# Summing key features against the context itself, and a new planner for the fills of two attention loops

## The chip, the cores and the metric

The kernel runs on one core of a Trainium2 chip. Times are device microseconds (us) of one execution. Five engines matter: TensorE (PE in the profile; its weight loads are PEld), VectorE (DVE), ScalarE (ACT), GpSimd (POOL) and the SyncE queue (SP), from which all DMAs are issued. Before the change three runs took 2615.45 to 2621.15 us, with a median of 2617.82.

## The reference

A perceiver of four levels: a stream x of 2 batches x 256 tokens x 256 features passes twelve blocks, some of which read a context of 2 x 4096 tokens x 256 features. Three blocks matter here.

`L0_xattn` and `L1_xattn` are ordinary cross attention with 16 heads of 16 features over all 4096 context tokens. They are where most of the time goes.

`L3_xattn` is linear attention of the stream on the same context:

```python
q, k, v = q @ Wq.T, k @ Wk.T, v @ Wv.T          # k and v are the context
q, k = focus(q), focus(k)                       # softmax(log(|leaky(x)|+eps) * factor) * mean
qh, kh = keep_11_largest_of_each_head_of_16(qh), ...(kh)
z_inv = einsum(qh, kh.mean(tokens)) + EPS
kv = einsum('bnc,bnd->bcd', kh / sqrt(n), vh / sqrt(n))
y = einsum('bnc,bcd->bnd', qh, kv) / z_inv
return y @ Wp.T
```

The keys' features of `L3_xattn` depend on the context and weights alone. So does kv, a sum over 4096 tokens of the product of the thinned key features and the values.

## The kernel before

Everything is fp32. The context's half of `L3_xattn` (class `Focus`) isn't computed in its own block but inside the two cross attention loops, one batch in each: `L0_xattn`'s loop does batch 0 and `L1_xattn`'s loop batch 1.

**A loop of steps.** `ContextAttention.attend` runs 8 units (2 batches x 4 groups of heads) of PER = 16 steps, and LAG and a last unit behind them, 148 steps in all. In step g PE does `first_scores` for one unit (L1018, eight PE instructions; DVE takes the maxima, L1026, two of 128 x 1024), then a **fill**, then `scores` for the unit 18 steps behind (L1042; ACT takes the exponents, L1052), then `weigh` of the step before (L1066). In steps 0 to 17 there are no second scores yet, in steps from 128 on no first ones. At the end of a unit, `weigh` copies the accumulator by DVE (L1075), and a step later `inverses` (L201) takes reciprocals.

**Banks.** PSUM in the loop has one bank for fills (`mm=1`), three pairs for scores (`sc=3`) and one accumulator. A step takes four pairs of the three in turn.

**Fills.** One step holds one fill at most: projecting keys (L939) or values (`v_ps`, L180), turning a unit's maxima (`shift_queries`, L994), normalising a unit, projecting one context tile of 128 tokens for `Focus` (`project`, L697: key features and values side by side, 512 columns), or adding up a chunk of four tiles (`add_up`, L710). `project` is followed by ACT (L609, and L701 which copies the values) and POOL (L610). When a chunk's four tiles are there, `Focus.weigh` takes the logarithm (ACT L617, POOL L618), the maximum (DVE L620), the exponents (L623) and a factor. Then `sparsify` ranks the 16 features of each head against each other: 15 shifts of one comparison (L648) and two additions (L650, L652) on DVE, then a select (L655) and a multiply by the factor (L660).

**Order.** PE, DVE and ACT follow the program's order here (`manual_schedule`). `plan` puts each fill into a step by due time, and holds for each step what DVE has left for ranking (`side`, 2.75 us with a fill, 2.0 without, minus what else falls there). `attend` hands out ranking instructions by that credit at the end of each step, behind `weigh`, `inverses` and the weighing. The sum of a chunk has a fixed step; if its ranking isn't over by then, all that is left of it is put out at once:

```python
if g in self.sums:
    run(rankings[self.sums[g]])
run(fills.get(g, ()))
```

The block `L3_xattn` (`l3_xattn`) does the same for its queries: projection, `weigh`, `sparsify`, transposes, then for each batch and half one product with kv and one with the features' sums, both masked to heads by `same`. It runs under the framework's own scheduling, not by program order.

Of the kernel before, what the change touches and what calls it, by code (L numbers as in the profile page):

```python
# [26 lines left out]
P = 128  # L27
# [556 lines left out]
class Focus:  # L584

    def __init__(self, net):
        self.net, self.nc = net, net.nc
        const, nc = net.const, net.nc  # L590
        src = net.ins["L3x_wkv"]
        self.wkv = const.tile(list(src.shape), F32, name="wkv", tag="wkv")
        nc.sync.dma_start(out=self.wkv, in_=src)
        self.power = net.vec("L3x_ff")
        self.eps = const.tile([P, 1], F32, name="eps6", tag="eps6")
        nc.gpsimd.memset(self.eps, 1e-6)
        self.rank0 = const.tile([P, P], BF16, name="rank0", tag="rank0")
        nc.gpsimd.iota(
            self.rank0, pattern=[[-1, DH], [0, H // ND]], base=DH - 1, channel_multiplier=0, allow_small_or_imprecise_dtypes=True
        )  # L600
        self.kv = [const.tile([P, ND, P + 1], F32, name=f"kv{b}", tag=f"kv{b}") for b in range(NB)]
# [30 lines left out]

    def sparsify(self, pool, y, factor):

# [9 lines left out]
        yield 0.42  # L644
        for s in range(1, DH):
# [3 lines left out]
            yield 0.13 + 1.18e-3 * N8 * n  # L649
            nc.vector.tensor_tensor(rank[:, :, P - n :], rank[:, :, P - n :], ge[:, :, :n], ALU.add)  # L650
            yield 0.13 + 0.62e-3 * N8 * n
            nc.vector.tensor_tensor(rank[:, :, :n], rank[:, :, :n], ge[:, :, :n], ALU.subtract)  # L652
            yield 0.13 + 0.62e-3 * N8 * n
# [4 lines left out]
        yield 1.22  # L658
        for t in range(NT):
            nc.vector.tensor_scalar_mul(y[:, t, :], y[:, t, :], factor[:, t : t + 1])  # L660
            yield 0.36


    def start(self, b, pool):
        self.b, self.pool, self.chunks, self.ctx, self.weighing = b, pool, [], [], []
        self.loads = iter([(kc, i) for kc in range(NKC) for i in range(2)])
        self.load()
# [11 lines left out]
    def project(self, kc, t):  # L679

        net, nc = self.net, self.nc
        if t == 0:
            y = self.pool.tile([P, NT, D], F32, name="fy", tag="fy")
            v = self.pool.tile([P, NT, ND, P + 1], F32, name="fv", tag="fv")
            nc.gpsimd.memset(v[:, :, :, P : P + 1], 1.0)
            total = net.sm(2, NT, name="f_total", tag="f_total")
            factor = net.sm(NT, name="f_factor", tag="f_factor")
            self.chunks.append((y, v, total, factor))
            self.weighing.append(self.weigh(y, total, factor))
        if t % 2 == 0:  # L690
            self.load()
        y, v, total, factor = self.chunks[kc]
        ctx = self.ctx[kc * 2 + t // 2]
        ps = net.mm("kv_ps")
        for d in range(ND):
            at = slice(t % 2 * P, (t % 2 + 1) * P)
            nc.tensor.matmul(ps, lhsT=ctx[:, d, at], rhs=self.wkv[:, d, :], start=d == 0, stop=d == ND - 1)  # L697
            if d < ND - 1:
                yield
        self.magnitudes(self.pool, y, total, t, ps[:, :D])  # L700
        nc.scalar.copy(v[:, t, :, :P], ps[:, D:].rearrange("p (m e) -> p m e", m=ND))  # L701

    def add_up(self, kc):

        nc = self.nc
        k, v, _, _ = self.chunks[kc]
        ps = self.net.mm("kv_sum")[:, : ND * (P + 1)].rearrange("p (m e) -> p m e", m=ND)
        for m in range(ND):
            for t in range(NT):
                nc.tensor.matmul(  # L710
                    ps[:, m, :], lhsT=k[:, t, m * P : (m + 1) * P], rhs=v[:, t, m, :], start=t == 0, stop=t == NT - 1
                )
            yield
        kv = self.kv[self.b]
        if kc == 0:
            nc.vector.tensor_copy(kv, ps)
        else:
            nc.vector.tensor_tensor(kv, kv, ps, ALU.add)


class ContextAttention:
# [73 lines left out]
    def plan(self):  # L795
# [6 lines left out]
        fills, todo, busy = {}, [], {}  # L802
        self.done = {}
        full, short = 2.75, 2.0
        side = [full] * STEPS
        for u in range(n):
            at = PER * (u + 1)
            fills[at] = self.shift_queries(u)
            side[at - 1] -= 0.3
            side[at] = short - 0.43  # L810
            at = PER * (u + 2) + LAG + 1
            self.done[at] = u
            side[at] -= 0.25
            if u < n - 1:
                fills[at + 1] = self.normalize(u)
                side[at + 1] = short - (0.43 if self.v_bias is None else 0.8)

        self.sums, self.weighings, self.rank_from = {}, {}, {}
        for kc in range(NKC):
            first = PER + 14 * kc + (2 if 2 * kc > NKC else 0)  # L820
            at = first + 28
            while at in fills:
                at += 1
            fills[at] = focus.add_up(kc)
            self.sums[at] = kc
            side[at] -= 0.45
            for t in range(NT):
                todo.append((first + 2 * t + 4, first + 2 * t + 1, focus.project(kc, t), kc))
        for j in range(self.begun, n * NKC // 2):
# [3 lines left out]
            last = max(4 * j - 8, 2 * i + PER + LAG + 1 if i >= 0 else 0)  # L833
            todo.append((4 * j - (5 if j < NKC // 2 else 3), last + 1, self.project_keys(j), -1))
        for b in range(NB):
            for kc in range(NKC):
                for k2 in range(2):
                    i = b * NKC + kc - self.VALUE_TILES
                    last = (i // NKC + 1) * NC16 * PER + LAG + 2 * (i % NKC) + 2 if i >= 0 else -1
                    first = (b * NC16 + 1) * PER + LAG + 2 * kc + k2  # L840
                    todo.append((first, last + 1, self.project_values(b, kc, k2), None))
        todo.sort(key=lambda t: t[0])
        for g in range((n + 1) * PER + LAG):

            ready = [t for t in todo if t[1] <= g and not (t[3] == busy.get(g - 1) == -1 and t[0] > g)]
            if g in fills or not ready:
                continue
            todo.remove(ready[0])
            assert ready[0][0] >= g, (g, ready[0])
            fills[g] = ready[0][2]  # L850
            busy[g] = ready[0][3]
        assert not todo


        for kc in range(NKC):
            done = max(g for g, of in busy.items() if of == kc)
            log = next((g for g in range(done + 1, done + 5) if g + 1 not in busy), done + 1)
            for behind in (0, 2, 3, 4, 5):
                self.weighings.setdefault(log + behind, []).append(kc)
            side[log + 2] -= 1.22  # L860
            side[log + 5] -= 0.65
            self.rank_from[kc] = log + 5
        for g in range(PER, STEPS):
            if g not in fills:
                side[g] += short - full
            if g >= n * PER:
                side[g] += 1.0
            if g >= 2 * PER + LAG and (g - PER - LAG - 1) % PER == PER - 1:
                side[g] -= 0.43
        self.side = side  # L870
        return fills

    def attend(self, vpool, ppool, fpool):
# [11 lines left out]
        rankings, ranked, credit = {}, 0, 0.0  # L885
        for g in range((n + 1) * PER + LAG + 2):
# [4 lines left out]
            if g in self.sums:  # L891
                run(rankings[self.sums[g]])
            run(fills.get(g, ()))
            if 0 <= second < n * PER:
# [9 lines left out]
            credit = min(credit, 0.5) + self.side[g]  # L904
            while ranked < NKC and self.rank_from[ranked] <= g:
                if ranked not in rankings:
                    y, _, _, factor = focus.chunks[ranked]
                    rankings[ranked] = focus.sparsify(fpool, y, factor)
                cost = next(rankings[ranked], None) if credit > 0.3 else 0.0
                if cost == 0.0:  # L910
                    break
                if cost is None:
                    ranked += 1
                else:
                    credit -= cost
# [1198 lines left out]
```

## Time and profile before

| what | value |
|---|---|
| median of three runs | 2617.82 us |
| the profiled execution | 2622.24 us, of which its span 2620.1 us |
| mean granted TensorE clock | 0.945 |
| busy shares of the span: PE, DVE, ACT, POOL | 90%, 61%, 41%, 13% |
| first loop, first scores of step 0 to first of step 127 | 35.9 to 675.1 us |
| second loop, the same | 999.5 to 1630.1 us |
| `project`, PE L697, both loops | 126.9 us busy in 256 instructions |
| `add_up`, PE L710, both loops | 34.4 us busy in 256 instructions |
| ranking, DVE L648, L650, L652 | some 400 us busy |

A PE instruction's own duration holds pipelining, so a group's busy time is more than the time it takes up on PE; the distance from one group's start to the next in the timeline is the better measure. A PE matmul in fp32 shows as two instructions. "Idle before" in a row tells how long the engine stood and who released it.

### The profile page before, as it was taken

What the parts mean: (1) busy time and instruction counts of PE and PEld (TensorE: products, weight loads), DVE (VectorE), ACT (ScalarE), POOL (GpSimd) and SP (SyncE); (2) the same over time, 40 slices, a digit from 0 to 9 for tenths busy, and PEclk for the clock granted to TensorE, in tenths of its full rate; (3) what the DMA queues carried; (4) which work ended last, traced back from release to release, by engine and by line L of the source; (5) the groups of instructions that cost most, each with busy time, mean ns of one, the idle gap of its engine ahead of it and who ended that gap; (6) DMA issues with size and microseconds to landing.
All of it is one profiled execution on the core that took longest, in us unless ns stands there. A gap on an engine that the chain in (4) does not pass through costs nothing.

```text
span 2620.1 us, 42454 instructions
## 1 busy us (share of the span) xinstructions
PE 2365.7 (90%) x16912; PEld 1222.9 (47%) x16920; DVE 1594.2 (61%) x2774; ACT 1069.4 (41%) x1891; POOL 332.8 (13%) x469
## 2 busy tenths in 40 slices
PE   7999999998998579999999999989999984789998
PEld 3444444544544354444445444554448442345453
DVE  4678888878846567488887788443231355434252
ACT  1355555555715132555555555531131352123241
POOL 3000011000024711000010000000011030002030
PEclk9999999999989789999999999978999996898989
DMA  5422222221010123322222220201222100000100
GB/s 184 141 82 86 66 78 82 70 79 57 2 37 33 46 81 120 99 82 74 70 79 91 75 72 18 80 13 49 85 97 89 37 17 13 33 20 12 51 16 20
DMA packets 89060, 165.99 MB, mean 63 GB/s; under 512 B 14704, under 2 KB 55280, under 8 KB 87968
## 3 DMA queue, kind: packets, MB, share of 16 engines
q1 hardware_dynamic: 88864, 163.29, 18.9%
q8 instruction: 134, 2.20, 0.3%
q14 instruction: 62, 0.51, 0.1%
HBM read 145.86 MB, written 0.59 MB: 56 GB/s over the span
## 4 chain that ended last, share of the span: by engine, by line
PE 49%; DVE 7%; ACT 2%; issue 1%; DMA 0%; POOL 0%; DVEq 0%; ACTq 0%; POOLq 0%
PE s L1042 5%; PE s L1018 5%; PE attn_acc L1066 5%; PE proj L180 4%; PE v_ps L180 3%; PE expert L180 2%; PE s L180 2%; PE kv_ps L697 2%; PE c_acc L1604 2%; PE ffn_ps L180 2%; PE k_ps L939 2%; DVE mx L1026 2%; PE s L1340 2%; PE kq_ps L180 1%; PE qk_ps L180 1%
## 5 line engine op out<-in xcount | busy, mean ns | idle before, releaser
L1026 DVE TENSOR_REDUCE mx<-s 128x2 f32<-128x1024 f32 x512 | 603.3, 1220 | 204.1 <-PE s L1018 202.6
L1052 ACT ACTIVATE p<-s 128x1024 f32<-128x1024 f32 x512 | 496.3, 1021 | 223.0 <-PE s L1042 219.0
L1042 PE MATMUL s<-xa_q,xa_k 32*128 32x256 f32 x4096 | 337.1, 405 | 36.9 <-DVE mx L1026 35.1
L1018 PE MATMUL s<-xa_k,xa_q 32*128 32x512 f32 x2048 | 350.7, 647 | 5.5 <-issue 2.8
L1042 PEld LDWEIGHTS s<-xa_q,xa_k 32*128 32x128 f32 x4096 | 207.4, 185 | 204.4 <-issue 118.5
L1066 PE MATMUL attn_acc<-p,xv 128*32 128x256 f32 x4096 | 278.9, 389 | 0.6 <-ACT p L1052 0.6
L1018 PEld LDWEIGHTS s<-xa_k,xa_q 32*128 32x128 f32 x2048 | 121.0, 185 | 123.5 <-issue 76.1
L648 DVE TENSOR_TENSOR ge<-fy 128x960 bf16<-128x960 f32 (+14 forms) x240 | 173.7, 724 | 6.4
L1066 PEld LDWEIGHTS attn_acc<-p,xv 128*32 128x32 f32 x4096 | 107.9, 109 | 132.2 <-issue 85.9
L610 POOL TENSOR_TENSOR fy<-fy,low 128x256 f32<-128x256 f32 x64 | 61.4, 960 | 697.0 <-ACT low L609 697.0
L697 PE MATMUL kv_ps<-wkv,f_ctx 128*128 128x512 f32 x256 | 126.9, 618 | 0.8 <-DVE xa_q L996 0.8
L650 DVE TENSOR_TENSOR rank<-rank,ge 128x960 bf16<-128x960 bf16 (+14 forms) x255 | 121.5, 476 | 6.8
L652 DVE TENSOR_TENSOR rank<-rank,ge 128x960 bf16<-128x960 bf16 (+14 forms) x255 | 111.3, 436 | 2.8
L387 POOL TENSOR_SCALAR p<-p,r 128x128 f32<-128x128 f32 (+1 forms) x192 | 82.5, 442 | 139.0 <-DVE r L383 76.2
L986 ACT COPY xv<-v_ps 128x512 f32<-128x512 f32 x64 | 37.5, 586 | 136.9 <-PE v_ps L180 127.0
L609 ACT ACTIVATE fy<-kv_ps 128x256 f32<-128x256 f32 x64 | 24.5, 383 | 149.9 <-PE kv_ps L697 149.9
L697 PEld LDWEIGHTS kv_ps<-wkv,f_ctx 128*128 128x128 f32 x256 | 43.3, 189 | 80.1 <-issue 71.4
L233 ACT ACTIVATE sq<-xc 128x512 f32<-128x512 f32 x24 | 14.6, 629 | 147.2 <-DVE xc L232 147.2
L368 ACT ACTIVATE p<-p,top 128x256 f32<-128x256 f32 (+1 forms) x128 | 57.1, 447 | 41.8 <-DVE top L356 39.0
L939 PE MATMUL k_ps<-ctx_k,w_L0x_wq 128*64 128x512 f32 x256 | 66.1, 619 | 3.0 <-DMA ctx_k<-in_ctxT 2.9
L1604 PE MATMUL c_acc<-pT,ctx_n 128*128 128x256 f32 x256 | 62.1, 387 | 4.2 <-ACT pT L1577 3.0
L180 PE MATMUL v_ps<-w_L0x_wv,ctx_v 128*128 128x256 f32 x256 | 63.8, 392 | 0.8 <-ACT k_dense L952 0.8
(444 smaller groups left out, 3339.6 us busy)
## 6 DMA issues: line engine op xcount, KB each, us to landing
ctx_k<-in_ctxT SPq DMA_DIRECT2D x128, 512.0 KB
ctx_v<-in_ctxT SPq DMA_DIRECT2D x64, 256.0 KB
xa_k<-k_dense SPq DMA_DIRECT2D x512, 32.0 KB
f_ctx<-in_ctxT SPq DMA_DIRECT2D x32, 256.0 KB
ctxT<-in_ctxT SPq DMA_DIRECT2D x16, 512.0 KB
ctx_n<-in_ctx SPq DMA_DIRECT2D x16, 512.0 KB
xa_k<-key_masks SPq DMA_DIRECT2D x128, 8.0 KB
w_L0f_w<-in_L0f_w SPq DMA_DIRECT2D x2, 1024.0 KB
```

Of the source, the lines that this page charges most:

```text
L180: self.nc.tensor.matmul(out, lhsT=lhsT, rhs=rhs, start=i == 0, stop=i == len(pairs) - 1)
L648: nc.vector.tensor_tensor(ge[:, :, :n], w[:, :, :n], w[:, :, P - n :], ALU.is_ge)
L650: nc.vector.tensor_tensor(rank[:, :, P - n :], rank[:, :, P - n :], ge[:, :, :n], ALU.add)
L652: nc.vector.tensor_tensor(rank[:, :, :n], rank[:, :, :n], ge[:, :, :n], ALU.subtract)
L697: nc.tensor.matmul(ps, lhsT=ctx[:, d, at], rhs=self.wkv[:, d, :], start=d == 0, stop=d == ND - 1)
L939: nc.tensor.matmul(ps[i * HR : (i + 1) * HR, :], lhsT=self.wk[:, d, c * HR : (c + 1) * HR], rhs=ctx[:, d, :], start=d == 0, stop=d == ND - 1,)
L1018: nc.tensor.matmul(pairs[i // 2][:, i % 2, :], lhsT=self.q[u][rows, qt * P : (qt + 1) * P], rhs=k[rows, :], start=True, stop=True,)
L1026: nc.vector.tensor_reduce(mx[:, qt, 2 * i : 2 * i + 2, kc], sc, AX.X, ALU.max)
L1042: nc.tensor.matmul(pairs[i // 2][:, i % 2, kk * S : (kk + 1) * S], lhsT=k[rows, at], rhs=self.q[u][rows, :], start=True, stop=True,)
L1052: nc.scalar.activation(p, sc, AF.Exp, scale=DH**-0.5)
L1066: nc.tensor.matmul(self.acc[i * HP : (i + 1) * HP, :S], lhsT=v[:, 2 * k2 + kk, at : at + HP], rhs=ps[i // 2][:, i % 2, kk * S : (kk + 1) * S],
L1604: nc.tensor.matmul(accs[m], lhsT=of[:, (k + i) % (KC // P), m * P : (m + 1) * P], rhs=pT[:, i, :], start=k + i == 0, stop=k + i == KT - 1,)
```

## The change

Four things:

1. **`L3_xattn` sums features times the context.** `project` makes the key features alone (256 columns). `add_up` multiplies the thinned features, not with values, but with the context's tokens themselves and a column of ones (257 columns, in two fills, one for each half of the features), and adds to `kc`. The tokens are a new tile of 512 KB a chunk, a single buffer, loaded by `load_tokens` when the first chunk begins and after the second half sum of each chunk. The values' projection is done once a batch, in `l3_xattn`, on the 256 x 256 sum: four transposes and four accumulated products for each batch.
2. **The planner.** Features have due times from step 5 on; two tiles of a chunk may go into one fill where due times press (`pressed`); key and value fills stay out of the step behind a chunk's logarithm; a sum waits until the ranking is over by the plan's own count and one more step; features of a chunk wait for the sums two chunks before. What each step gets of ranking is worked out in the plan (`self.rankings`).
3. **Ranking ahead of weighing.** `attend` puts out a step's ranking right behind its fill, ahead of the second scores, the copy of the accumulator, `inverses` and `Focus.weigh`.
4. The multiply by the factor goes from DVE to POOL.

The diff, cut to its core:

```diff
-        src = net.ins["L3x_wkv"]
+        src = net.ins["L3x_wk"]
...
-        self.kv = [const.tile([P, ND, P + 1], F32, name=f"kv{b}", tag=f"kv{b}") for b in range(NB)]
+        self.kc = [const.tile([P, ND, D + 1], F32, name=f"kc{b}", tag=f"kc{b}") for b in range(NB)]
...
+    def costs(self):
+        n = lambda s: NT * ND * (DH - s) * (H // ND)
+        of = lambda s: [0.13 + 1.18e-3 * n(s), 0.13 + 0.62e-3 * n(s), 0.13 + 0.62e-3 * n(s)]
+        return [0.42, *(c for s in range(1, DH) for c in of(s)), 1.22]
...
         for t in range(NT):
-            nc.vector.tensor_scalar_mul(y[:, t, :], y[:, t, :], factor[:, t : t + 1])
-            yield 0.36
+            nc.gpsimd.tensor_scalar(y[:, t, :], y[:, t, :], factor[:, t : t + 1], 1.0, ALU.mult, ALU.mult)
+        yield
...
+        self.tokens = pool.tile([P, NT, D + 1], F32, name="f_tok", tag="f_tok", bufs=1)
+        self.nc.gpsimd.memset(self.tokens[:, :, D : D + 1], 1.0)
...
+    def load_tokens(self):
+        kc = next(self.token_loads, None)
+        if kc is not None:
+            src = self.net.ins["ctx"][self.b, kc * KC : (kc + 1) * KC].rearrange("(t p) d -> p t d", p=P)
+            self.nc.sync.dma_start(out=self.tokens[:, :, :D], in_=src)
...
-    def project(self, kc, t):
+    def project(self, kc, first, n=1):
...
-        ps = net.mm("kv_ps")
-        for d in range(ND):
-            at = slice(t % 2 * P, (t % 2 + 1) * P)
-            nc.tensor.matmul(ps, lhsT=ctx[:, d, at], rhs=self.wkv[:, d, :], start=d == 0, stop=d == ND - 1)
-        self.magnitudes(self.pool, y, total, t, ps[:, :D])
-        nc.scalar.copy(v[:, t, :, :P], ps[:, D:].rearrange("p (m e) -> p m e", m=ND))
+        ps = net.mm("f_ps")
+        for i in range(n):
+            t = first + i
+            if t % 2 == 0:
+                self.load()
+            ctx = self.ctx[kc * 2 + t // 2]
+            at = slice(t % 2 * P, (t % 2 + 1) * P)
+            net.matmuls(ps[:, i * D : (i + 1) * D], [(ctx[:, d, at], self.wk[:, d, :]) for d in range(ND)])
+        for i in range(n):
+            self.magnitudes(self.pool, y, total, first + i, ps[:, i * D : (i + 1) * D])
...
-    def add_up(self, kc):
+    def add_up(self, kc, m):
+        ps = self.net.mm("kc_sum")[:, : D + 1]
+        self.net.matmuls(ps, [(k[:, t, m * P : (m + 1) * P], self.tokens[:, t, :]) for t in range(NT)])
+        yield
+        kc_sum = self.kc[self.b][:, m, :]
+        if kc == 0:
+            nc.vector.tensor_copy(kc_sum, ps)
+        else:
+            nc.vector.tensor_tensor(kc_sum, kc_sum, ps, ALU.add)
+        if m == ND - 1:
+            self.load_tokens()
...
+        for kc in range(NKC):
+            first = 5 + 31 * kc // 2
+            todo += [(first + 2 * t + 4, first + t, ("features", kc, t)) for t in range(NT)]
+            todo += [(first + 30 + m, first + 14, ("sums", kc, m)) for m in range(ND)]
...
+        def ready(g, deadline, earliest, which):
+            kind, kc, *_ = which
+            if earliest > g or (g in logs and kind != "sums" and deadline > g):
+                return False
+            if kind == "keys":
+                return kinds.get(g - 1) != kind or deadline <= g
+            if kind == "features":
+                return kc < 2 or not any(w[:2] == ("sums", kc - 2) for _, _, w in todo)
+            return kind != "sums" or over.get(kc, g) + 1 < g
+
+        def pressed(g):
+            for n, (deadline, _, _) in enumerate(todo):
+                if n + 1 + sum(g < f <= deadline for f in fixed) > deadline - g:
+                    return True
+            return False
+
+        for g in range(STEPS):
+            room = short
+            t = None if g in fills else next((t for t in todo if ready(g, *t)), None)
+            if t is not None:
...
+                if kind == "features":
+                    kc, tile = which
+                    if tile + 1 < NT and pressed(g):
+                        fills[g] = focus.project(kc, tile, 2)
+                        room, tile = full, tile + 1
+                    if tile == NT - 1:
+                        for behind in (0, 2, 3, 4, 5):
+                            self.weighings.setdefault(g + 1 + behind, []).append(kc)
+                        logs.add(g + 2)
+                        taken[g + 3] += 1.22
+                        taken[g + 6] += 0.65
+                        begin[kc] = g + 7
+                else:
+                    room = full
+                    taken[g] += 0.42 * (kind == "sums")
+            if g < PER:
+                room = 0.5
+            if g >= last + 1:
+                room = 2.2
+            credit = min(credit, 0.5) + room - taken[g]
+            while ranked < NKC and begin.get(ranked, STEPS) <= g and credit > 0.3:
+                self.rankings.setdefault(g, []).append(ranked)
+                credit -= costs[at]
...
             run(self.beginning)
-            if g in self.sums:
-                run(rankings[self.sums[g]])
             run(fills.get(g, ()))
+            for kc in self.rankings.get(g, ()):
+                if kc not in rankings:
+                    y, _, factor = focus.chunks[kc]
+                    rankings[kc] = focus.sparsify(fpool, y, factor)
+                run(rankings[kc], 1)
             if 0 <= second < n * PER:
                 self.scores(second // PER, second % PER)
...
-    wq, wp = net.load("L3x_wq", "L3x_wp")
+    wq, wv, wp = net.load("L3x_wq", "L3x_wv", "L3x_wp")
...
+        kvs = []
+        for b in range(NB):
+            turned = work.tile([P, ND, ND, P], F32, name="kcT", tag="kcT")
+            for m in range(ND):
+                net.from_tokens(lambda d, k: turned[:, m, d : d + k], focus.kc[b][:, m, :D], ND)
+            ps = net.acc("kv_ps")
+            for m in range(ND):
+                at = slice(m * P, (m + 1) * P)
+                net.matmuls(ps[:, at], [(turned[:, m, d, :], wv[:, d, at]) for d in range(ND)])
+            kvs.append(ps)
...
-                of = focus.kv[b][:, m, :]
-                nc.vector.scalar_tensor_tensor(kv, same, NK / S, of[:, :P], ALU.mult, ALU.mult)
-                nc.vector.tensor_scalar_mul(km, same, of[:, P : P + 1])
+                of = kvs[b][:, m * P : (m + 1) * P]
+                nc.vector.scalar_tensor_tensor(kv, same, NK / S, of, ALU.mult, ALU.mult)
+                nc.vector.tensor_scalar_mul(km, same, focus.kc[b][:, m, D : D + 1])
```

## The prediction

> **What bounds the kernel now.** I read the table of windows over the two attention loops first, then the timeline of single steps, then the lines around each unit's end, then the groups.
>
> ```profile
> core 0: us, PE busy (x) PEld busy (x) DVE busy (x) ACT busy (x) POOL busy (x), PEclk, DMA share, GB/s
> 93.00:675.00 582.00, 560.68 (x5066) 269.55 (x5064) 457.48 (x644) 318.29 (x504) 45.87 (x51) 0.98 0.23 75
> 1053.00:1630.00 577.00, 555.28 (x5057) 266.98 (x5056) 455.84 (x638) 315.15 (x503) 45.83 (x51) 0.99 0.23 74
> ```
>
> PE is busy 96% of both loops, DVE 79%, ACT 55%, DMA 23%. So the loops are PE's, with DVE close behind. How a step divides shows in two steps, one with a fill and one without:
>
> ```profile
> 1291.35 1.37 PE L1018 MATMUL s<-xa_k,xa_q 32*128 32x512 f32 x8
> 1292.65 1.98 PE L697 MATMUL kv_ps<-wkv,f_ctx 128*128 128x512 f32 x4
> 1294.56 1.15 PE L1042 MATMUL s<-xa_q,xa_k 32*128 32x256 f32 x16
> 1295.64 1.07 PE L1066 MATMUL attn_acc<-p,xv 128*32 128x256 f32 x16
> 1296.64 1.37 PE L1018 MATMUL s<-xa_k,xa_q 32*128 32x512 f32 x8
> ```
>
> ```profile
> 1630.07 1.14 PE L1018 MATMUL s<-xa_k,xa_q 32*128 32x512 f32 x8
> 1631.03 0.60 PE L1042 MATMUL s<-xa_q,xa_k 32*128 32x256 f32 x4
> 1632.53 1.13 PE L1042 MATMUL s<-xa_q,xa_k 32*128 32x256 f32 x12 [0.90 <-DVE mx L1026]
> 1633.59 1.07 PE L1066 MATMUL attn_acc<-p,xv 128*32 128x256 f32 x16
> 1634.59 0.44 PE L994 MATMUL top_ps<-ident,xa_top 128*128 128x128 f32 x2
> ```
>
> The filled step lasts 5.29 us and PE never stops; 1.91 of it (1292.65 to 1294.56) is the projection, 512 columns by two halves. The empty step lasts 4.52, not 5.29 - 1.91 = 3.38: the second score group needs a third pair of banks, which the first maximum of DVE must free, so PE stands 0.90 us. **A fill's first 0.9 us or so are free; the rest is paid.** The step starts of both loops give medians of 5.27 for filled steps and 4.55 for steps that are empty or hold only the short shift.
>
> The rest is lost where a unit of 16 steps ends, and once in a burst:
>
> ```profile
> 1143.16 0.42 DVE L1075 COPY a<-attn_acc 128x256 f32<-128x256 f32 x1 [1.53 <-PE attn_acc L1066]
> 1149.83 0.21 DVE L201 RECIPROCAL inverses<-sums 128x8 f32<-128x8 f32 x1 [1.63 <-PE sums L180]
> 1153.56 1.13 PE L1042 MATMUL s<-xa_q,xa_k 32*128 32x256 f32 x12 [1.50 <-DVE mx L1026]
> 1579.75 3.10 PE L710 MATMUL kv_sum<-fv,fy 128*128 128x129 f32 x14 [2.29 <-DVE fy L660]
> ```
>
> DVE stands waiting for PE with its ranking work queued behind the wait, then does it late, and the next maxima come late: PE pays 1.50. The last line is a sum whose ranking had not been finished in time.
>
> **The sum by parts.** Profiled execution: 2622.2, its span 2620.1, 2.1 around it; the median of the runs, 2617.8, lies 4.4 below. Savings are worked on the span and taken from the median.
>
> Fills. A tile's projection falls from 512 columns to 256: 1.91/2 = 0.955 us, 3.33 + 0.955 = 4.29 for PE, below the 4.55 that an empty step takes. A feature step alone is therefore priced as an empty step, 4.55; a doubled one as before, 5.27. A sum goes from eight matmuls of 129 columns (1.98, from 1340.56 to 1342.54) to two fills of four matmuls of 257: like the values' fill of 4 x 256, 1.92 each, so two filled steps. Keys and values are unchanged, 61 or 62 fills a layer. Applying both texts of plan() step by step, the 110 steps from 18 to 127 hold:
>
> - layer 0: before 83 filled and 27 light; after 66 filled (24 values, 25 keys, 13 half sums, 4 doubled) and 44 light (20 single features among them);
> - layer 1: before 82 and 28; after 67 and 43.
>
> At 5.27 and 4.55 that is 560.3 and 559.5 before, 548.0 and 548.8 after. The measured stretches (93.4 to 680.0 and 1053.1 to 1635.0) are 586.7 and 581.8, so **26.4 and 22.3 us are excess** over the two step prices.
>
> Excess. Summed from the step starts of layer 1: 14.3 at unit ends and 4.0 at the burst of step 117, some 4 at the Ln steps. Each unit end needs 0.54 more on PE (L180 sums) in any case; where no ranking fell there (steps 83/84, 99/100), that was all it cost. With ranking emitted ahead of the copy of acc and the inverses, DVE works during those waits: I take 6 x 0.54 + 6 x 0.3 = 5. The burst goes: the new plan starts a sum only two steps after its ranking. The Ln steps I put at 2.5, since the step behind is now kept empty except for sums (two do fall there), against about 1.1 each before where it was filled. Doubled features (two tiles through ACT and the single `low`) 1.2, DVE's adds behind sums 1.4, and for steps 18 and 19, where the second scores begin, with the unassigned rest 2.4. Sum 12.5; bounds 5 and 26.
>
> So the middles go 586.7 to 560.5 (-26.2) and 581.8 to 561.3 (-20.5).
>
> Start, steps 0 to 17 (57.4 and 53.7). Features move in at 0.955 against a step that DVE's two maxima hold at 2.4, and push out values' fills of 3.0: -1.8 and -3.0. But ranking now starts at step 15 or 17, where the second scores have not begun: steps 16 and 17 took 5.85 together, and get 2.0 and 2.6 (0 and 3.1) on top of two maxima of 1.22 each: +3.5 and +1.7. Net +1.7 and -1.3.
>
> Tail: layer 0 has three half sums there (5.8 against 4.0), and in both the last sum can wait a little: +2.5 and +0.7.
>
> DVE and POOL. Ranking is 26.1 us a chunk by the plan's own costs. The multiply by factor leaves DVE, 64 x 0.347 (L660), and becomes 4 x 0.478 on POOL (L387 has the shape), 13% busy. The planner gives ranking 2.0 and 2.75 of DVE in light and filled steps, beside 2.28 for the two maxima (642.04 to 644.32 in the timeline), so that the 22 us count only where steps are light; I give them nothing of their own. A second add of 0.42 per chunk comes back. ACT loses 64 x 0.373 (L701), which hid behind PE: 0. POOL's ones for v go: 0.
>
> [...]
>
> ```profile
> 1279.83 1.04 POOL L610 TENSOR_TENSOR fy<-fy,low 128x256 f32<-128x256 f32 x1 [11.31 <-ACT low L609]
> 1280.31 1.38 DVE L648 TENSOR_TENSOR ge<-fy 128x768 bf16<-128x768 f32 x1
> ```
>
> The same shape took 0.95 at 1649.61, in the tail, clear of POOL: 0.4 lost here. [...] But in the plan at least two steps without ranking follow each chunk's end save one, and the scaling falls there[...]. I take 0[...].
>
> DMA. The tokens add 16 loads of 512 KB, 8.4 MB; at 23% share with ten or more steps between load and use they are covered. On SP's queue each waits for the second half sum; behind it stand later keys' loads, which are due steps afterwards. If that cover were gone, a late load would hold PE some 3 us (512 KB at the start's 183 GB/s). The first two fall where SP and DMA are fullest (share 0.57), with the early f_ctx load: +2 in layer 0, between 0 and 6. The half as large weight load at the very start gives -1 (256 KB at 184 GB/s is 1.4; PE waits there for ctx_k).
>
> L3. Values' projection: eight transposes (q's eight took 2.0) and eight matmul pairs of 128 columns (some 2.2), four copies. DVE ranks q for 26 us with PE idle 33.6, which could hide them; but they stand ahead of q's projection in the program. Between 0 and 6; I take +2.
>
> Together: -26.2 - 20.5 + 1.7 - 1.3 + 2.5 + 0.7 + 2 - 1 + 2 = **-40**, so 2617.8 - 40 = **2578 us**.
>
> **Rivals.** (1) *Excess stays*: ranking ahead of weighing only moves DVE's lateness, doubled features stall ACT, POOL's adds hit full DVE steps. Excess then 24 a layer, +23: 2601. For it: a light step leaves DVE 4.55 - 2.28 - 2.0 = 0.27, less than one meeting with POOL (0.4). Against: steps 83 to 100. (2) *The gap isn't usable*: a single feature costs its 0.955 on top of 4.55; 40 steps x 0.955 = 38: 2616, no change. Against it: PE's own sum is 4.29 and its wait is in the very place where the fill goes. (3) *Slower: sums wait for POOL.* In the plan every first half sum comes two steps after its ranking's last piece; that leaves DVE's last select and POOL's four scalings about 10 us, of which they need some 6 to 9. PE runs in order, so a late scaling holds all scores. Above 2.5 us for each of 16 chunks the gain is gone; 4 us gives 2578 + 64 = 2642. POOL's adds of this size were seen at up to 1.6 us beside DVE, and four of those would be 6.4. (4) *Better*: excess 5 a layer, L3 hidden: 2560.
>
> **How the numbers follow.** My forecast 0.60, spread 2563 to 2592; (1) 0.20; (2) 0.04; (3) 0.08; (4) 0.08. The range 2556 to 2608 takes in my own, (1) and (4) and leaves out (2), (3) and their neighbourhood. What a measurement can tell from no change is 0.2%, 5 us. Faster 0.89 (my forecast, (1), (4) and a little of (2)), same 0.03 (the rest of (2)), slower 0.08 (3).
>
> **What would show it.** Right: single-feature steps near 4.55 without the 0.90 wait at the second scores; the middles near 561; no idle DVE before L1075's copy as long as 1.5 beside queued ranking; no wait of a sum for scaling. Wrong: waits of the sums' matmuls on POOL; waits for the tokens' DMA; the wait on mx kept in feature steps; ACT's waits grown in doubled ones; L3's projection ahead of a standing PE.

## The result and the profile after

The changed kernel takes **2580.1 us** (median of four runs, 2571.9 to 2584.3) against 2617.3 before (four runs): a ratio of 0.985, 95% interval 0.9825 to 0.988. The medians lie 37.2 us apart. The forecast was 2578, range 2556 to 2608.

The profiled span falls by 40.1, from 2620.1 to 2580.0; of the executions before, the profiled one was 4.4 us slower than the median. By stretches, from the starts of the steps in both traces (the tail is what a loop does from step 128 on):

| stretch | before | after | forecast | measured |
|---|---|---|---|---|
| up to layer 0's first scores | 35.9 | 34.1 | -1 | -1.8 |
| layer 0: steps 0-17 / 18-127 / tail | 57.4 / 586.7 / 42.6 | 57.0 / 560.5 / 44.2 | +1.7 / -26.2 / +2.5 | -0.4 / -26.2 / +1.6 |
| layer 0: DMA of tokens | | | +2 | none |
| layer 1: steps 0-17 / 18-127 / tail | 53.7 / 581.8 / 42.6 | 50.6 / 564.5 / 42.5 | -1.3 / -20.5 / +0.7 | -3.1 / -17.3 / -0.1 |
| `L2_attn`, code unchanged | 120.2 | 126.0 | 0 | +5.8 |
| `L3_xattn` | 68.4 | 69.9 | +2 | +1.5 |
| all other blocks | 1030.8 | 1030.7 | 0 | -0.1 |

The windows over steps 18 to 127 of both loops, of the changed kernel (columns: window, length, busy time and instructions of each engine, granted clock, DMA share, GB/s):

```profile
core 0: us, PE busy (x) PEld busy (x) DVE busy (x) ACT busy (x) POOL busy (x), PEclk, DMA share, GB/s
91.10:651.60 560.50, 545.87 (x5128) 279.43 (x5126) 460.26 (x645) 307.21 (x459) 49.27 (x68) 1.00 0.26 84
1022.90:1587.30 564.40, 549.11 (x5136) 281.14 (x5134) 459.50 (x643) 304.57 (x459) 48.58 (x68) 0.99 0.26 83
```

PE is still busy 97% of the loops and DVE 82%: they are PE's, as before, only shorter. Its granted clock is higher, 1.00 and 0.99 against 0.98 and 0.99; that turns out to matter. The profile's groups show what PE now does for `L3_xattn`:

```profile
L1077 PE MATMUL s<-xa_q,xa_k 32*128 32x256 f32 x4096 | 337.7, 402 | 22.9 <-DVE mx L1061 20.9
...
L180 PE MATMUL f_ps<-f_wk,f_ctx 128*128 128x256 f32 x256 | 70.0, 401 | 1.2 <-ACT low L610 1.2
...
L180 PE MATMUL kc_sum<-f_tok,fy 128*128 128x257 f32 x256 | 64.2, 393 | 0.0
```

and the group of the second scores before:

```profile
L1042 PE MATMUL s<-xa_q,xa_k 32*128 32x256 f32 x4096 | 337.1, 405 | 36.9 <-DVE mx L1026 35.1
```

`project` went from 126.9 us busy to 70.0 (its 256 instructions last 401 ns each, 102.7 us together, so they overlap), the sums from 34.4 to 64.2, and PE's wait for the maxima at the second scores from 35.1 to 20.9. One step with a single feature tile, in PE's timeline:

```profile
1138.35 1.29 PE L1053 MATMUL s<-xa_k,xa_q 32*128 32x512 f32 x8
1139.57 1.13 PE L180 MATMUL f_ps<-f_wk,f_ctx 128*128 128x256 f32 x4
1140.63 1.44 PE L1077 MATMUL s<-xa_q,xa_k 32*128 32x256 f32 x16
1142.00 1.07 PE L1101 MATMUL attn_acc<-p,xv 128*32 128x256 f32 x16
1143.00 1.14 PE L1053 MATMUL s<-xa_k,xa_q 32*128 32x512 f32 x8
```

From first scores (1138.35) to first scores (1143.00) are 4.65 us, and the next such step takes 4.52 (to 1147.52); the median of the 20 in each loop is 4.52. The wait of 0.90 at the second scores is gone: the projection stands in its place. The end of a unit, DVE and PE:

```profile
1193.81 1.03 DVE L654 TENSOR_TENSOR ge<-fy 128x832 bf16<-128x832 f32 x1
...
1194.75 0.42 DVE L1110 COPY a<-attn_acc 128x256 f32<-128x256 f32 x1
1195.44 2.36 DVE L1061 TENSOR_REDUCE mx<-s 128x2 f32<-128x1024 f32 x2 [0.27 <-PE s L1053]
...
1197.49 1.15 PE L1077 MATMUL s<-xa_q,xa_k 32*128 32x256 f32 x16
...
1200.72 0.21 DVE L201 RECIPROCAL inverses<-sums 128x8 f32<-128x8 f32 x1 [0.39 <-PE sums L180]
...
1202.62 1.60 PE L1077 MATMUL s<-xa_q,xa_k 32*128 32x256 f32 x16
```

The copy (L1110) finds its sum ready, because a comparison (L654) ran in the time that DVE used to wait; `inverses` waits 0.39, where L1075 and L201 waited 1.53 and 1.63; and the second scores come without a wait on the maxima. Last, who the sums' instructions waited for, from the list of the tokens' tile:

```profile
L180 PE MATMUL kc_sum<-f_tok,fy x256: 377/380/484, 151.7 to 1620.8; 128*128 128x257 f32 x128
...
its engine sat idle before it (us, times) until:
...
  POOL fy L665: 0.4, 1
```

256 instructions of the sums waited once for the scaling on POOL, 0.4 us, and never for the tokens' DMA.

### The profile page after: what moved, and what is told of

Its sections match the earlier page's. It is cut to its first block, busy times and chain, and to the rows that moved or that the text cites. A ratio compares the mean times of both kernels' runs of the same rounds, so it can differ in the third digit from the quotient of the medians.

```text
span 2580.0 us, 42414 instructions
## 1 busy us (share of the span) xinstructions
PE 2340.7 (91%) x16936; PEld 1243.8 (48%) x16944; DVE 1577.8 (61%) x2724; ACT 1054.5 (41%) x1829; POOL 352.6 (14%) x523
## 4 chain that ended last, share of the span: by engine, by line
PE 78%; DVE 11%; ACT 5%; issue 3%; POOL 2%; DMA 1%; SPq 0%; ACTq 0%; DVEq 0%; POOLq 0%
PE s L1053 11%; PE s L1077 10%; PE attn_acc L1101 9%; PE v_ps L180 6%; PE proj L180 5%; PE k_ps L974 4%; DVE mx L1061 3%; PE kc_sum L180 2%; PE expert L180 2%; PE s L180 2%; PE f_ps L180 2%; PE c_acc L1639 2%; PE ffn_ps L180 2%; PE s L1375 2%; PE o L411 1%
## 5 line engine op out<-in xcount | busy, mean ns | idle before, releaser
L1077 PE MATMUL s<-xa_q,xa_k 32*128 32x256 f32 x4096 | 337.7, 402 | 22.9 <-DVE mx L1061 20.9
L654 DVE TENSOR_TENSOR ge<-fy 128x960 bf16<-128x960 f32 (+14 forms) x240 | 172.9, 720 | 6.2
L611 POOL TENSOR_TENSOR fy<-fy,low 128x256 f32<-128x256 f32 x64 | 50.3, 787 | 792.8 <-ACT low L610 792.8
L180 PE MATMUL f_ps<-f_wk,f_ctx 128*128 128x256 f32 x256 | 70.0, 401 | 1.2 <-ACT low L610 1.2
L180 PEld LDWEIGHTS f_ps<-f_wk,f_ctx 128*128 128x128 f32 x256 | 44.1, 189 | 46.7 <-issue 27.3
L180 PE MATMUL kc_sum<-f_tok,fy 128*128 128x257 f32 x256 | 64.2, 393 | 0.0
```

Source lines behind the costliest of these rows:

```text
L180: self.nc.tensor.matmul(out, lhsT=lhsT, rhs=rhs, start=i == 0, stop=i == len(pairs) - 1)
L654: nc.vector.tensor_tensor(ge[:, :, :n], w[:, :, :n], w[:, :, P - n :], ALU.is_ge)
L1077: nc.tensor.matmul(pairs[i // 2][:, i % 2, kk * S : (kk + 1) * S], lhsT=k[rows, at], rhs=self.q[u][rows, :], start=True, stop=True,)
```

## What the half clock did

One thing the forecast had no term for. Windows of the kernel before, around a unit's end in layer 0:

```profile
core 0: us, PE busy (x) PEld busy (x) DVE busy (x) ACT busy (x) POOL busy (x), PEclk, DMA share, GB/s
...
610.00:612.50 2.50, 0.32 (x4) 0.00 (x0) 2.40 (x8) 0.54 (x3) 0.00 (x0) 1.00 0.48 156
612.50:614.50 2.00, 1.88 (x24) 1.13 (x28) 1.20 (x2) 1.04 (x2) 0.00 (x0) 0.92 0.10 25
614.50:620.50 6.00, 6.00 (x47) 3.34 (x42) 3.73 (x13) 0.90 (x1) 0.00 (x0) 0.50 0.02 4
```

and two lines of its timeline there:

```profile
612.62 1.13 PE L1042 MATMUL s<-xa_q,xa_k 32*128 32x256 f32 x12 [2.30 <-DVE mx L1026]
...
616.05 2.09 PE L1018 MATMUL s<-xa_k,xa_q 32*128 32x512 f32 x8
```

PE stands 2.30 us for a maximum; 1.6 us later its clock is granted at 0.50 for 6.8 us, and the first scores, 1.37 elsewhere, take 2.09. Adding up (1 - granted clock) over steps 18 to 127, the middle of each loop, gives what a middle lost: **before, the two middles lost 10.2 and 5.1 us to half clock, after it 0 and 3.4.** Each dip in the middles is 3.4 or 6.8 us long. In the twelve profiles of this study (before, after and ten experiments) the middles hold 68 waits of PE of 1.1 us or more. With 30 of them a dip began during the wait or within 4.5 us of its end, stretches that make up some 3% of the time; three further dips followed the 0.9 wait of step 18, and none came without such a wait. So a wait that is removed seems to spare, now and then, 1.7 or 3.4 us (half of such a dip) more than its own length; that the wait causes the dip is read from this sequence and was not tried by itself. Net of it the middles go from 576.5 and 576.7 to 560.5 and 561.1, and the two layers, which seemed to differ, agree: 16.0 and 15.6 us gained.

Half clock also accounts for `L2_attn`, whose instructions are the same ones. The windows before, then after:

```profile
2030.00:2150.00 120.00, 111.64 (x524) 58.48 (x525) 55.27 (x251) 50.63 (x160) 26.99 (x65) 0.97 0.06 21
```

```profile
1981.50:2107.50 126.00, 117.91 (x524) 61.57 (x525) 55.17 (x251) 50.73 (x160) 27.03 (x65) 0.92 0.06 22
```

524 PE instructions each time, DVE and ACT equal to 0.1 us, but the clock at 0.92 against 0.97: the block lost 10.2 us to half clock against 3.4. It takes 120.3 to 121.0 us in eight of the ten experiments, seven of them variants of the changed kernel, 122.9 in e5, but 124.8 in e0, which is the changed kernel itself. Net of half clock it is 115.8 to 117.8 in all twelve profiles. So the 5.8 us are the clock's; that the changed kernel lost them in both of its profiles may be chance, and these runs don't settle it.

## Experiments

Each edit is to the changed kernel unless said otherwise. "Net" is steps 18 to 127 of layers 0 and 1 in the one profile of each kernel, less the time lost to half clock. The last column uses all runs: the mean of span times granted clock. It is an index of the time without half clock, not a time (it also takes off half clock that cost nothing because PE stood), and runs of one kernel differ less in it (standard deviation 0.6 to 3.3 us) than in their spans (2.5 to 6.3).

| kernel | median us | ratio to before, 95% | net | span x clock |
|---|---|---|---|---|
| before | 2616.2 to 2617.1 | 1 | 576.5, 576.7 | 2477.0 to 2477.9 |
| e0_after | 2578.6 | 0.9857 (0.9831 to 0.9884) | 560.4, 560.8 | 2442.3 |
| e1_rank_behind | 2594.7 | 0.9925 (0.9901 to 0.995) | 570.1, 571.7 | 2464.3 |
| e2_before_rank_ahead | 2594.0 | 0.9915 (0.9897 to 0.9933) | 570.5, 569.3 | 2465.9 |
| e3_wide_features | 2609.7 | 0.9971 (0.996 to 0.9981) | 575.6, 576.5 | 2477.9 |
| e4_double_all | 2610.4 | 0.9979 (0.9971 to 0.9987) | 576.4, 574.9 | 2480.0 |
| e5_no_table | 2559.2 | 0.9783 (0.9756 to 0.9809) | 552.6, 554.0 | 2428.6 |
| e6_dve_scale | 2582.5 | 0.9876 (0.9856 to 0.9897) | 562.3, 563.6 | 2449.2 |
| e7_better | 2577.1 | 0.985 (0.9823 to 0.9877) | 559.8, 560.7 | 2442.7 |
| e8_no_rule | 2570.4 | 0.9807 (0.9785 to 0.9829) | 555.2, 556.6 | 2435.7 |
| e9_rule_later | 2563.7 | 0.9804 (0.9784 to 0.9825) | 556.9, 557.8 | 2438.2 |

The runs come from three chips, each with runs of the kernel before beside them: e0, e1, e3 and e4 from one, e2, e5, e6 and e7 from another, e8 and e9 from a third.

**e0: the changed kernel again**, beside e1, e3 and e4 on their chip.

> The changed kernel itself once more, as the base for the others of the same chip. My theory (fills ride in the gap of light steps, ranking ahead of weighing takes back the waits at unit ends, no burst): loop middles 560.5 and 564.5 us again, the same to 0.5. If the 5.8 us that the second-level attention block lost at a lower granted clock was chance, that block is near 120 here with a clock near 0.97; if the change brought it, it is 126 again.

2578.6. Layer 0's middle missed the 560.5 that was expected: in its profile step 19 lasts 3.3 us longer than in the one above, because the granted clock is 0.50 from 99.1 to 105.9 us, behind step 18's wait of 0.94. Net, 560.4 and 560.8 repeat the 560.5 and 561.1. `L2_attn` took 124.8, not near 120.

**e1: ranking behind weighing, as it was.**

```diff
             run(fills.get(g, ()))
-            for kc in self.rankings.get(g, ()):
-                ...
             if 0 <= second < n * PER:
                 self.scores(second // PER, second % PER)
...
             for kc in self.weighings.get(g, ()):
                 run(focus.weighing[kc], 1)
+            for kc in self.rankings.get(g, ()):
+                ...
```

> The changed kernel with each step's ranking put out behind the weighing again, the plan and all else as changed. My theory: DVE stands again before the copy of acc and before the reciprocals with ranking queued behind, 1 to 2 us at each of 12 unit ends that have ranking; the middles grow by 7 to 10 us each, the whole by 14 to 20. Rival (the order is worth nothing, all of the gain is PE work saved): within 4 us of the changed kernel.

16 us slower than e0, within what was expected; the middles lose 9.7 and 10.9 net, at the unit ends, which is more than 16 together: by span times clock e1 is 22.0 slower, and its runs were granted more clock than e0's (0.950 against 0.948 in the mean), in `L2_attn` for one. DVE and PE at one of them:

```profile
1208.21 0.21 DVE L201 RECIPROCAL inverses<-sums 128x8 f32<-128x8 f32 x1 [1.63 <-PE sums L180]
1208.34 0.54 DVE L656 TENSOR_TENSOR rank<-rank,ge 128x832 bf16<-128x832 bf16 x1
...
1210.41 2.35 DVE L1061 TENSOR_REDUCE mx<-s 128x2 f32<-128x1024 f32 x2
...
1211.69 1.13 PE L1077 MATMUL s<-xa_q,xa_k 32*128 32x256 f32 x12 [1.24 <-DVE mx L1061]
```

DVE stands 1.63 for `inverses` with ranking queued behind it, does that ranking at 1208.34 to 1210.4, and its maximum comes late enough to hold PE 1.24. In the changed kernel the same place cost nothing.

**e2: the kernel before, with ranking ahead of weighing alone.**

```diff
             run(fills.get(g, ()))
+            (ranking by credit, as it stood at the end of the step)
             if 0 <= second < n * PER:
                 self.scores(second // PER, second % PER)
```

> The kernel before with one thing changed: each step's ranking put out behind the fill, ahead of the second scores and the weighing. My theory: the waits at unit ends go (14.3 us of excess in the second middle, of which 4.0 stand at step 115, beside the burst, and 3.2 are PE's own work), the burst of step 117 stays: 6 to 9 us in each loop, 12 to 18 faster than before. Rival (order is worth nothing): within 4 us of before.

22 to 23 us faster than before, more than expected. Net, the middles gain 6.0 and 7.4, which is the gain that was expected (the unit ends, which lost 14.3 together in layer 1, keep 0.51 to 0.56 each, as PE's own `sums` needs); another 10.2 is half clock that no longer comes in the middles (15.3 to 5.1). By span times clock the order alone is worth 12 us here. The burst at step 117 stays: 5.5 and 4.1, half clock in it included. It is the planner that removes it.

**e3: features of full width**, so that a single tile's fill again has 512 columns.

```diff
+            if n == 1:
+                net.matmuls(ps[:, D:], [(ctx[:, d, at], self.wk[:, d, :]) for d in range(ND)])
```

> The changed kernel with each single-tile feature fill made 512 columns wide again by a second pair of matmuls on the same data, whose result is not used; the plan is unchanged. My theory (0.9 us of PE gap in a light step, so that 0.955 is free and 1.91 is not): a single-feature step of the middles goes from 4.52 to 5.27, 20 steps in each, 15 us each; with the start steps the whole grows by 30 to 36 us. Rival A (every fill costs its own PE time wherever it stands): 46 fills times 0.955, 44 us. Rival B (the steps are DVE's, PE work is covered anyway): under 8 us.

31 us slower than e0, as expected. PE's timeline of the feature step behind the one shown above:

```profile
1164.18 1.31 PE L1055 MATMUL s<-xa_k,xa_q 32*128 32x512 f32 x8
1165.42 1.99 PE L180 MATMUL f_ps<-f_wk,f_ctx 128*128 128x256 f32 x8
1167.34 1.15 PE L1079 MATMUL s<-xa_q,xa_k 32*128 32x256 f32 x16
1168.42 1.07 PE L1103 MATMUL attn_acc<-p,xv 128*32 128x256 f32 x16
1169.42 1.31 PE L1055 MATMUL s<-xa_k,xa_q 32*128 32x512 f32 x8
```

5.24 us against 4.52 (median 5.30), and no wait anywhere: the second half is paid for in full. This settles that the first half lies in the gap and costs nothing.

**e4: all features doubled.**

```diff
-                    if tile + 1 < NT and pressed(g):
+                    if tile % 2 == 0:
```

> The changed kernel with all feature tiles put in pairs, two to a fill: the same matmuls in fewer and fuller fills, with as many more empty steps. My theory (a single feature is free in the gap, a pair pays 0.72, and ACT is late behind a pair): 10 more filled and fewer light steps in each middle, 7 us each for PE and up to 5 for ACT; the whole grows by 14 to 24 us. Rival (a fill costs its PE time wherever it stands): no change, within 4 us.

32 us slower than e0, more than expected. Fourteen doubled fills a loop take 5.07 to 5.30 away from the unit ends and leave 22 or 23 steps empty at 4.52, so the gap goes unused: 5.24 + 4.52 for a pair against 2 x 4.52 is 0.72, and ten more pairs than in the changed kernel make 7.2 a loop. Net, 16.0 and 14.1 were lost. Most of the rest falls into eight steps behind doubled fills (24, 38, 40, 54, 70, 86, 102, 114), which take 0.9 to 1.2 us more each. Step 38 of layer 0, which would take 5.24, in PE's timeline:

```profile
203.28 1.13 PE L1053 MATMUL s<-xa_k,xa_q 32*128 32x512 f32 x4
204.67 1.13 PE L1053 MATMUL s<-xa_k,xa_q 32*128 32x512 f32 x4 [0.25 <-ACT p L1087]
...
209.67 1.31 PE L1053 MATMUL s<-xa_k,xa_q 32*128 32x512 f32 x8
```

The first scores stop half way for ScalarE's exponents, and the step takes 6.39: two tiles at once make the exponents late. I had underrated that.

**e5: no table switching for the chunks.** Exp takes the place of the logarithm, so the features aren't the reference's; all else is the same.

```diff
-        nc.scalar.activation(y, y, AF.Ln, bias=self.eps)
+        nc.scalar.activation(y, y, func, bias=self.eps)
...
-            self.weighing.append(self.weigh(y, total, factor))
+            self.weighing.append(self.weigh(y, total, factor, AF.Exp))
```

> The changed kernel with the logarithm of each key chunk replaced by an exponential of the same shape, so that ACT loads no table there; the features of the keys are therefore not those of the reference. My theory: the 1.2 us lost two steps behind each chunk's logarithm are ACT's two table loads (1.28 each) that make the exponents and then the second pair of first scores late; they go, 5 or 6 in each middle, the whole is 9 to 17 us faster than the changed kernel. Rival (that step is late for DVE's maximum of the features, 1.21 us, which stays): within 4 us of it.

19 us faster than e0, a little more than expected; net 7.8 and 6.8 in the middles. In the changed kernel the second step behind a chunk's logarithm is 1.1 to 1.3 us longer than others of its kind, six times in each middle; here those steps are ordinary. So the table loads cost some 15 us in the middles, where the forecast had 2.5 a loop. That agrees with span times clock, 13.7. How, in ACT's and PE's timeline of the changed kernel:

```profile
1153.65 1.28 ACT L618 ACT_TABLE_LOAD   x1
...
1154.95 1.15 ACT L618 ACTIVATE fy<-fy,eps 128x1024 f32<-128x1024 f32 x1
...
1156.12 1.28 ACT L1087 ACT_TABLE_LOAD   x1
...
1157.05 1.13 PE L1053 MATMUL s<-xa_k,xa_q 32*128 32x512 f32 x4
1157.41 1.94 ACT L1087 ACTIVATE p<-s 128x1024 f32<-128x1024 f32 x2
...
1158.49 1.13 PE L1053 MATMUL s<-xa_k,xa_q 32*128 32x512 f32 x4 [0.31 <-ACT p L1087]
...
1159.55 1.99 PE L180 MATMUL v_ps<-w_L1x_wv,ctx_v 128*128 128x256 f32 x8
...
1161.47 1.15 PE L1077 MATMUL s<-xa_q,xa_k 32*128 32x256 f32 x16
...
1163.55 1.36 PE L1053 MATMUL s<-xa_k,xa_q 32*128 32x512 f32 x8
```

Two loads of 1.28 around a logarithm of 1.15 put the next exponents (1157.41) late; the first scores of the step need their bank, stop half way (the second half starts 1.44 behind the first, where 0.53 is usual), and the values' fill follows with everything behind it. The step takes 6.50 instead of 5.30.

**e6: multiply by the factor back on DVE.**

```diff
-            nc.gpsimd.tensor_scalar(y[:, t, :], y[:, t, :], factor[:, t : t + 1], 1.0, ALU.mult, ALU.mult)
+            nc.vector.tensor_scalar_mul(y[:, t, :], y[:, t, :], factor[:, t : t + 1])
```

> The changed kernel with the multiply by factor back on DVE. My theory (at a chunk's end DVE has steps without ranking, the multiply is free on either engine): 0 to 4 us slower. Rival A (ranking fills DVE, 64 times 0.347 us count): 15 to 22 slower. [...]

4 us slower than e0, with intervals that overlap; net +1.9 and +2.8, and 6.9 more by span times clock. So the move to POOL is worth some 5 us, not the 0 of the sum.

**e7: values' projection moved behind the queries' ranking in the program, no doubled tile at a unit's end, and little ranking up to step 17** (the moved block is left out here).

```diff
-                    if tile + 1 < NT and pressed(g):
+                    if tile + 1 < NT and g not in self.done and pressed(g):
-            if g < PER:
+            if g < PER + LAG:
```

> Three small edits to the changed kernel: the values' projection stands behind the ranking of the queries in L3_xattn instead of ahead of their projection; no doubled feature in a step that ends a unit; ranking gets 0.5 us a step up to step 17 instead of 15. My theory: 2 us in L3 (PE idles there while DVE ranks), 0.7 at each of 6 unit ends, some 1 in each start: 4 to 10 us faster than the changed kernel. Rival: within 2 us of it.

1.4 us faster than e0: no difference that can be told, and less than expected. Little ranking up to step 17 does help: steps 18 and 19 together take 10.3 in each layer, against 12.6 in the changed kernel. The unit ends fall to 0.51, but the doubled fills only move, and steps 54, 70 and 86, behind them, take 0.9 to 1.4 more. In `L3_xattn` the time from the mean's matmuls to the first product with kv is 47.4 before, 49.5 after and 48.2 here: what stood ahead of the queries was worth some 1.3 us there. The whole block still takes 69.8 against 69.9, since behind that product 10.5 us went to half clock instead of 7.8.

**e8 and e9: where the empty step of a logarithm lies.** e8 lets keys and values into the step behind it; e9 keeps the second step behind it free instead.

```diff
-            if earliest > g or (g in logs and kind != "sums" and deadline > g):
+            if earliest > g:
```

> The changed kernel, but key and value fills may also go into the step behind a chunk's logarithm. In the changed kernel that step is empty, and still the step after it is 1.2 us late. Theory: ScalarE sets the pace there. A step's two exponents (2.04), one logarithm (1.15) and two table loads (1.28 each) make 5.75 us against an empty step's 4.55, so 1.2 is left over whatever TensorE does; a fill in that place is hidden, the lateness falls to about 0.5, and 12 Ln places give 0.7 each: about 8 us faster than the changed kernel (some 2570 in the medians, middles 556). Rival: the lateness is added to whatever TensorE has in that step, as the kernel before suggests, where filled steps behind Ln lost 1.1: then nothing changes, 2575 to 2583 and middles of 560.5 and 561, net of half-clock time.

```diff
-                        logs.add(g + 2)
+                        logs.add(g + 3)
```

> The changed kernel, but the step that is kept free of key and value fills is the second one behind a chunk's logarithm, where the lateness of 1.2 us shows, and no more the first. Theory that ScalarE sets the pace: TensorE waits in that step anyway, so taking its fill away only makes the wait longer (1.9), while the fill that moves into the step ahead is hidden: between 0 and 8 us faster. Rival, lateness added to TensorE's own work: no change, middles of 560.5 and 561 net of half-clock time.

Both are faster than the changed kernel, by 8 and 15 us in the medians, though e8's interval still touches that of the changed kernel's first four runs (0.9825 to 0.988). Their ratios to `before` are the same, so neither can be called the faster. Net, the middles gain 9.4 together in e8 and 6.5 in e9, and by span times clock they gain 6.6 and 4.1: the rest of e9's 15 us is clock. The number for e8 was met, its reason was not: the second step behind a logarithm is 1.1 to 1.3 late there too, with a fill in the step ahead of all but the last. Its gain is another one: with more places for fills only 1 tile in a loop is doubled instead of 4, and the middle has 62 and 63 filled steps for 66 and 67; 4 x 0.72, and some 0.6 at each of two unit ends that no longer hold a doubled tile, is 4.1 of the 4.7 a loop. In e9 the lateness vanishes for three of the chunks in layer 0 and two in layer 1. ACT and PE of e9 in the step that answers to the one above:

```profile
1150.90 1.13 PE L1053 MATMUL s<-xa_k,xa_q 32*128 32x512 f32 x4
...
1151.35 1.94 ACT L1087 ACTIVATE p<-s 128x1024 f32<-128x1024 f32 x2
...
1152.42 1.13 PE L1053 MATMUL s<-xa_k,xa_q 32*128 32x512 f32 x4 [0.39 <-ACT p L1087]
...
1153.34 1.27 PE L1077 MATMUL s<-xa_q,xa_k 32*128 32x256 f32 x16
...
1155.54 1.24 PE L1053 MATMUL s<-xa_k,xa_q 32*128 32x512 f32 x8
```

The first scores stop for the exponents as before (0.39). But the step is empty, so PE would have stood anyway until DVE's first maximum; that maximum is over meanwhile, the second scores start at once, and the step takes 4.64. **An empty step's 0.9 us can be spent once, on half a fill or on ScalarE's lateness**, and the step that pays for the tables is the second, not the first behind them. Where a sum falls into that step (30, 91 and 108, and 74 in layer 1), 1.1 to 1.3 is still lost, as in step 30 of layer 1, which takes 6.59:

```profile
1081.80 1.13 PE L1053 MATMUL s<-xa_k,xa_q 32*128 32x512 f32 x4 [0.39 <-ACT p L1087]
1082.85 2.01 PE L180 MATMUL kc_sum<-f_tok,fy 128*128 128x257 f32 x8
```

The wait of 1.9 that e9's expectation had for an empty step came nowhere.

## Why the prediction was right

- **Gap and fill prices held.** 5.24 to 5.31 for filled steps, 4.52 for single features against the 4.55 used; e3 gives the other half its full price of 0.7 to 0.8. Rival (2) is out.
- **The middles: 560.5 and 561.3 forecast, 560.5 and 561.1 net measured, but this agreement is partly luck.** The forecast took them from 586.7 and 581.8, with half clock in them, and so promised 46.7 us; net, the change gained 31.6. The excess left is 12.5 in layer 0, as forecast, made otherwise. Ln steps: 7.3 measured for 2.5; the step that fell to emptiness was the wrong one (e9). Unit ends and doubled tiles: 5.1 for 6.2. Steps 18 to 21: 3.0 for 2.4. The step at the last logarithm: 0.4. The remaining steps lie 3.3 below their price, where I had added 1.4 for DVE's additions; keys' steps next to an empty one take 5.02.
- **The excess before was misread.** Of 26.4 and 22.3 us, 10.2 and 5.1 were half clock, among them part of what I called unit ends and burst. Most of it went along with the long waits in the profiled execution, so that the sum came out. Over all runs less of the gain is clock: by span times clock the changed kernel is 2443.4 in the first four runs, 34.5 below the kernel before, where the forecast had 40 and the medians gave 37.2.
- **Ranking ahead does what the forecast said:** e1 and e2 give 16 and 22 us for the order alone, and 22 and 12 by span times clock. Rival (1), that it moves lateness only, is out.
- **Start:** -0.4 and -3.1 for +1.7 and -1.3. The ranking that was to lengthen steps 16 and 17 left them as they were (5.81 together, 5.85 before). Its cost fell behind the line: steps 18 and 19 take 12.6 together against 10.4 before, and e7, with less ranking there, brings them to 10.3. **Tail:** +1.6 and -0.1 for +2.5 and +0.7. **First load:** -1.8 for -1.
- **DMA:** no wait for the tokens, so +2 was too careful. **L3:** +1.5 for +2.
- **Rival (3), sums waiting for POOL:** 0.4 us once in the kernel, with the 64 scalings at 0.479 each. The plan's step between ranking and sum was enough. The scaling's move itself, put at 0, was worth some 5 us (e6).
- **Errors that cancelled:** against the sum the starts gave 3.9 us more, the tokens 2.0, the tails 1.7, the first load 0.8 and L3 0.5; layer 1's middle gave 3.2 less (3.4 of it half clock) and `L2_attn` took 5.8. That is 8.9 against 9.0, in one pair of executions; `L2_attn`'s part in it is clock, and luck.

## What to carry to other kernels

In a software pipeline, price a step by the engine that ends it, find the gap that the dependencies leave in it, and decide what to spend that gap on: here half a projection is free, a whole one costs 0.7, and an empty step placed where another engine is late was worth 1.2 in five places. Queue work that waits for nothing ahead of an instruction that waits, not behind it: the order alone was worth 16 and 22 us here (e1, e2). And before a profile's lost time is put down to waits, subtract what the granted clock took: a wait may bring a stretch of half clock behind it, as 30 of 68 did here, with 3.4 or 6.8 us at 0.50, and that stretch does not come in every run: step 18's wait brought one in e0 (99.1 to 105.9 us) and none in the profile of the changed kernel above, whose layer 0 lost nothing.

## What was not expected of the hardware

Waits of PE of 1.1 to 2.8 us in a loop that keeps it 96% busy came in 30 of 68 cases with 3.4 or 6.8 us at a granted clock of 0.50, during the wait or just behind it. In the traces before and after alone it was 8 of 15: in layer 0 before, a wait of 2.30 that ended at 612.62 had 6.8 us of it behind it, while one of 1.34 in layer 1 after, ended at 1549.49, had none. What decides whether a given wait is followed by a dip isn't shown by these runs. Switching ScalarE's tables for one logarithm cost two loads of 1.28 us, 1.2 us of which reached PE two steps later, 12 times in the two middles.
